# Self attention's output projections of seven token blocks: four products of four 128 by 128 by 512 matmuls, or seven half-size products combined in place

## The chip, the cores and the metric

The kernel runs on one core of one Trainium2 chip. The metric is the device time of one execution in microseconds (us); lower is better. All arithmetic is float32.

## The reference, cut to what matters

The program is an encoder over a short context (77 tokens), then a decoder layer over x of shape (2, 2048, 512) with 16 heads of 32. The step that changes is the output projection of the decoder's causal self attention, with its residual:

```
yn = _ln(y, dec_n1_s, dec_n1_b)
y = y + _mha(yn, yn, dec_sa_in_w, dec_sa_in_b, dec_sa_out_w, dec_sa_out_b, sb)
...
out = jnp.einsum('bhqk,bhkd->bhqd', attn, v)
out = out.transpose(0, 2, 1, 3).reshape(Bq, Tq, D)
return out @ w_out.T + b_out
```

So 2 x 2048 rows of attention output, 512 wide, are multiplied by a 512 by 512 weight; a bias row and the residual y are added. After it come cross attention and a feed-forward layer.

## The kernel before, in words

**Blocks and units.** The 4096 tokens are eight blocks of 512, written (b, m): batch b in 0..1 and m in 0..3; here they are also called block 0 to 7. A block's self attention is 16 units: four groups g of four heads, and in each group four tiles t of 128 query tokens. A unit of block m has 4m+t+1 key tiles. It is worked through by `scores` (L374 matmuls into PSUM banks; VectorE copies the scores out with a running maximum, L383, and adds the bias near the diagonal, L390; L399 makes the negated maximum), `exps` (ScalarE, L404), `turn` (TensorE transposes, L424, copied out by ScalarE, L430, or VectorE, L428) and `values` (L452). Scores of a unit are computed up to two units ahead.

**Order.** Nothing is scheduled by a tool: each engine runs its instructions in the order of the program text. At the start of unit n the function `slot(n)` emits, in this order, the closures in `light[n]`, the jobs in `jobs[n]`, then those in `late[n]`. Jobs are TensorE products: q (`q_job`, L215), k and v of each block, and the output projection. Light and late work is normalisation, loads and GpSimd sums. Every load and store is issued by SyncE's queue (SP), in program order; a load that waits for its buffer holds up all later ones. `load_next` fetches a job's weights ahead, at most three in the ring `wqk` of three 256 KB buffers.

**Half-size products, already there.** For blocks with m > 0, k and v are made not by four full products but by seven products of half-size factors (`part_job`, L1024 to L1063): one 256 by 256 quarter of the weight, or a sum of quarters made once (`wc_sums`, `wc_store`, kept in DRAM as `sa_k`, `sa_v`), times one quarter of the block's 512 by 512 input or a sum of quarters (T1 to T4, made by GpSimd in `token_sums`, L956). Each product is four matmuls of 256 columns (L1038) into one bank, and its result is copied or added into one or two quarters of the output.

**The output projection.** `out_job(b, m, t)` (L246 to L257) takes the weight held in the 1 MB tile `wbt` and the block's four oT tiles (one per group; 512 features by 512 tokens altogether; GpSimd has divided them by the softmax sums at L489). It makes one tile of 128 tokens: four matmuls of 512 columns (L251), one VectorE add of the residual tile (L254), one store (L255). The residual tile was loaded (L262) and had the bias row `bo` added by GpSimd (L266) a unit before. Block x's four out jobs stand in units 6, 7, 8, 9 of the next block (7 to 10 where the next block starts a batch); those of the last block come after the units. `wbt` holds v's full weight for the first block of each batch and the output weight otherwise. `fold_job` (L1065) folds v's bias through the output weight into `bo`, once, in block 1.

**Neighbours in the same units.** Units 5 to 8 load the normalisation input of the block after next (`norm_load`, tag xt, two buffers, L275); unit by unit GpSimd scales it (`norm_center`, L286, L293) and TensorE transposes it (`norm_turn`, L305). In block 2 GpSimd also makes sums of feed-forward weights (`w2_sums`, L956 on `pp`), in block 6 of others; in blocks 4 and 5 the first block's cross attention is woven in (`first_cross`).

Of the kernel before, what the change touches and what calls it, by code (L numbers as in the profile page):

```python
# [10 lines left out]
F32 = mybir.dt.float32  # L11
AF = mybir.ActivationFunctionType
ALU = mybir.AluOpType
# [4 lines left out]
P = 128  # L18
# [36 lines left out]
def tile_encoder_decoder(ctx: ExitStack, tc: tile.TileContext, ins, out):  # L55
# [103 lines left out]
    with (  # L159
# [34 lines left out]
        nTs, qTs, ots, sums_of = {}, {}, {}, {}  # L194
        wbig, xs, xr = {}, {}, {}

# [38 lines left out]
        def v_job(b, m, t):  # L235
            def run(w):
                mm = bank()
                for c in range(NC):
                    nc.tensor.matmul(
                        mm, nTs[b, m][:, c, ts(t, P)], w[:, c, :], start=(c == 0), stop=(c == NC - 1)  # L240
                    )
                nc.vector.tensor_copy(vv[:, m * TB + t, :], mm)

            return lambda: big_w("v"), run, False

        def out_job(b, m, t):  # L246
# [9 lines left out]

            return lambda: big_w("o"), run, False  # L257

# [178 lines left out]
        def values(pair):  # L437
# [18 lines left out]
            if keep:  # L456
                return
            if (b, m, g) not in ots:
                ots[b, m, g] = in_turn("oT", oT_all)
            o = ots[b, m, g]  # L460
# [529 lines left out]

        sa_d = {k: dram.tile([4, P, D], F32, name=f"sa_{k}", tag=f"sa_{k}") for k in "kv"}
        sa_from = {"k": D, "v": 2 * D}
        kstep = sm.tile([P, 2], F32, name="kstep", tag="kstep", bufs=1)
# [13 lines left out]
        def token_sums(b, m):  # L1007
# [3 lines left out]
            for name in ("T1", "T2", "T3", "T4"):  # L1011
                sum_n(name, lambda n: of_nT(b, m, n))

        def part_job(kind, b, m, i):
            name, by = PARTS[i]

            def load():
                w = sb.tile([P, NC, P], F32, name="wqk", tag="wqk", bufs=3).rearrange("p c o -> p (c o)")
                w = w.rearrange("p (c o) -> p c o", c=2)
                if name[0] == "S":  # L1020
                    src = sa_d[kind][int(name[1]) - 1].rearrange("p (c o) -> p c o", c=2)
                else:
                    src = quarter("dec_sa_in_wT", int(name[1]) - 1, int(name[0]) - 1, sa_from[kind])
                nc.sync.dma_start(w, src)  # L1024
# [61 lines left out]
        for x, (b, m) in enumerate(blocks):  # L1086
# [28 lines left out]
            for t in range(TB):  # L1115
                end = x == len(blocks) - 1
                out_at = u + NU + (2 if end else 7 if m == NMB - 1 else 6) + t
                jobs[out_at].append(out_job(b, m, t))
                if not end:
                    (light if x else late)[out_at - 1].append(lambda b=b, m=m, t=t: residual(b, m, t))  # L1120
                elif t < 2:
                    light[u + NU - 1].append(lambda b=b, m=m, t=t: residual(b, m, t))
                if x:
                    held = x == 1 and t >= 2
# [141 lines left out]
        light[len(units) - 5].append(early_loads)  # L1266
        light[len(units) - 1].append(last_loads)


# [576 lines left out]
```

## Time and profile before

| what | value |
|---|---|
| three runs, us | 2768.12, 2771.48, 2767.57; median 2768.12 |
| profiled execution, us | 2771.65 |
| its span, first to last instruction, us | 2769.9 |
| granted TensorE clock, mean | 0.995 |
| TensorE busy / VectorE / ScalarE / GpSimd, us | 2724.6 / 1807.0 / 1538.8 / 915.6 |
| SP's dynamic DMA queue | 358.18 MB, 41.4% of 16 engines' span |

How to read it: PE is TensorE's matmuls, PEld its weight loads, DVE VectorE, ACT ScalarE, POOL GpSimd, SPq the DMA queue of SyncE. A float32 matmul shows as two records. A group line gives source line, engine, operation, output<-input, shapes, the number of records, busy us, mean ns of one, and the idle time before them with what ended it. A timeline line gives start in us, length in us, engine, line, operation and count; idle time and its releaser stand in brackets. Records of matmuls overlap: the length of one is not the time for which it holds the engine; that is read from start to start.

### The profile page before, as it was taken

The page shows a single profiled execution, that of the slowest core. Times are in us where ns is not written, and L with a number is a line of the kernel's source. Part 1 is how long each engine was busy: PE and PEld are TensorE (multiplying, and loading weights), DVE is VectorE, ACT ScalarE, POOL GpSimd, SP SyncE. Part 2 cuts the span into 40 slices and gives each one's busy share as a digit, 9 for nine tenths or more (in the row PEclk, how much of TensorE's full clock was granted, in tenths as well). Part 3 has the DMA queues.
Part 4 walks back from the last instruction along what each step waited for, and adds up shares of the span by engine and source line. Part 5 has one row for each costly group of instructions (what it writes and reads, how often), then busy time and mean ns, then how long its engine had stood idle before and what let it go on. Part 6 is the DMA issues. An engine that isn't in the chain of part 4 may idle for free.

```text
span 2769.9 us, 67113 instructions
## 1 busy us (share of the span) xinstructions
PE 2724.6 (98%) x26294; PEld 2154.4 (78%) x26294; DVE 1807.0 (65%) x5312; ACT 1538.8 (56%) x2993; POOL 915.6 (33%) x777
## 2 busy tenths in 40 slices
PE   9999999999999999999999999999999999999998
PEld 5577776677776567676677777898989898989898
DVE  5775587787776587677687783556464646464645
ACT  3444567667777557677667786444444444444431
POOL 1501135300100413213200003364646464646456
PEclk9999999999999999999999999999999999999999
DMA  8433345311112422233211004565657564656465
GB/s 225 141 97 113 106 124 178 118 55 48 47 40 70 130 78 68 72 100 115 95 50 35 29 29 158 184 227 160 225 160 239 170 223 162 222 162 222 148 225 183
DMA packets 282254, 362.47 MB, mean 131 GB/s; under 512 B 39072, under 2 KB 156624, under 8 KB 281810
## 3 DMA queue, kind: packets, MB, share of 16 engines
q1 hardware_dynamic: 281938, 358.18, 41.4%
q8 instruction: 208, 3.41, 0.5%
q14 instruction: 108, 0.88, 0.1%
HBM read 314.49 MB, written 43.59 MB: 129 GB/s over the span
## 4 chain that ended last, share of the span: by engine, by line
PE 89%; DVE 4%; ACT 3%; issue 1%; POOL 1%; DMA 1%; SPq 0%; POOLq 0%; DVEq 0%; ACTq 0%
PE psum L424 17%; PE psum L1516 14%; PE psum L1545 12%; PE psum L374 9%; PE psum L452 8%; PE psum L1038 4%; PE psum L251 4%; PE psum L215 4%; PE psum L1676 3%; PE psum L1633 3%; ACT pp L404 3%; DVE pp L383 2%; PE psum L860 2%; PE psum L830 1%; PE psum L868 1%
## 5 line engine op out<-in xcount | busy, mean ns | idle before, releaser
L404 ACT ACTIVATE pp<-pp,nm 128x128 f32<-128x128 f32 (+15 forms) x512 | 611.8, 1201 | 34.5 <-DVE nm L399 34.0
L383 DVE TENSOR_SCALAR_CACHE_REDUCE pp<-psum 128x512 f32<-128x512 f32 (+3 forms) x1024 | 555.5, 591 | 75.0 <-PE psum L374 73.4
L424 PE MATMUL psum<-ident,pp 128*128 128x128 f32 x4352 | 536.4, 278 | 20.2 <-ACT pp L404 13.5
L430 ACT COPY pts<-psum 128x512 f32<-128x512 f32 (+2 forms) x736 | 386.5, 580 | 298.9 <-PE psum L424 258.0
L424 PEld LDWEIGHTS psum<-ident,pp 128*128 128x128 f32 x4352 | 478.5, 142 | 79.4 <-issue 24.9
L374 PE MATMUL psum<-kT,q 32*128 32x512 f32 (+3 forms) x2560 | 321.6, 559 | 4.6 <-ACT nT L310 2.6
L452 PEld LDWEIGHTS psum<-pts,vv 128*32 128x32 f32 x8704 | 226.7, 110 | 122.5 <-DVE pp L383 67.5
L428 DVE COPY pts<-psum 128x512 f32<-128x512 f32 (+3 forms) x400 | 249.5, 654 | 106.6 <-PE psum L424 104.4
L1545 PE MATMUL psum<-pp 128*128 128x128 f32 x2560 | 304.5, 276 | 1.9 <-POOL pp L956 1.6
L1545 PEld LDWEIGHTS psum<-pp 128*128 128x128 f32 x2560 | 296.3, 192 | 8.6 <-issue 2.8
L452 PE MATMUL psum<-pts,vv 128*32 128x128 f32 x8704 | 279.5, 276 | 6.7 <-DVE pp L383 4.2
L956 POOL TENSOR_TENSOR pp<-pp 128x512 f32<-128x512 f32 x159 | 212.6, 1354 | 126.5 <-DMA pp<-in_dec_ff_wT_dram 66.5
L1516 PE MATMUL psum<-vv,pp 128*128 128x256 f32 x1024 | 236.2, 381 | 0.0
L374 PEld LDWEIGHTS psum<-kT,q 32*128 32x128 f32 x2560 | 138.4, 183 | 125.6 <-issue 53.6
L1516 PEld LDWEIGHTS psum<-vv,pp 128*128 128x128 f32 x1024 | 190.3, 190 | 25.8 <-issue 0.5
L390 DVE CUSTOM_DVE_ANT_0 pp<-psum,bias 128x256 f32<-128x256 f32 (+1 forms) x512 | 196.2, 411 | 13.8 <-PE psum L374 13.6
L1529 DVE TENSOR_TENSOR kT<-kT,psum 128x512 f32<-128x512 f32 x96 | 65.8, 686 | 191.1 <-PE psum L1516 190.9
L1516 PE MATMUL psum<-nT,pp 128*128 128x256 f32 x768 | 174.1, 380 | 0.0
L1532 ACT ACTIVATE kT<-kT,vecs 128x256 f32<-128x256 f32 x192 | 87.0, 501 | 156.6 <-DVE kT L1529 155.9
L489 POOL TENSOR_TENSOR oT<-rirows,oT 128x512 f32<-128x512 f32 x30 | 38.4, 1280 | 377.9 <-DMA rirows<-rec 269.8
L1516 PEld LDWEIGHTS psum<-nT,pp 128*128 128x128 f32 x768 | 144.2, 190 | 20.3 <-issue 1.6
L266 POOL TENSOR_TENSOR xr<-xr,row_dec_sa_out_b 128x512 f32<-128x512 f32 x30 | 38.2, 1274 | 352.9 <-DMA xr<-in_x_dram 304.9
(243 smaller groups left out, 3907.5 us busy)
## 6 DMA issues: line engine op xcount, KB each, us to landing
pp<-w_d SPq DMA_DIRECT2D x520, 256.0 KB
pp<-in_dec_ff_wT_dram SPq DMA_DIRECT2D x112, 256.0 KB
wqk<-in_dec_sa_in_wT_dram SPq DMA_DIRECT2D x76, 256.0 KB
bias<-tzg SPq DMA_DIRECT2D x128, 128.0 KB
pp<-wo_d SPq DMA_DIRECT2D x56, 256.0 KB
vv<-in_enc_ff_wT_dram SPq DMA_DIRECT2D x8, 1024.0 KB
xr<-in_x_dram SPq DMA_DIRECT2D x32, 256.0 KB
vv<-y SPq DMA_DIRECT2D x32, 256.0 KB
```

The source lines that it names most:

```text
L215: nc.tensor.matmul(mm, w[:, c, :], nTs[b, m][:, c, :], start=(c == 0), stop=(c == NC - 1))
L374: nc.tensor.matmul(banks[r][:, : kn * P], q[rows4(r), ts(t, P)], kT[rows4(r), g, k0 * P : (k0 + kn) * P], start=True, stop=True,)
L383: nc.vector.tensor_scalar(p[:, k0 : k0 + far], s[:, :far], 1.0, None, ALU.mult, ALU.max, accum_out=st["mx"][:, r, c : c + 1],)
L390: nc.vector.tensor_tensor_reduce(p[:, k0 + far : i + 1], s[:, far:kn], near[:, 2 - (kn - far) :], 1.0, LOWEST, ALU.add, ALU.max, accum_out ...
L404: nc.scalar.activation(p, p, AF.Exp, bias=nm, accum_out=to)
L424: nc.tensor.transpose(pt[:, ts(x, P)], state[n]["p"][r][:, k], ident)
L428: nc.vector.tensor_copy(pts[:, : len(load), :], pt[:, :w])
L430: nc.scalar.copy(pts[:, : len(load), :], pt[:, :w])
L452: nc.tensor.matmul(ot[rows4(r)], vv[:, k, ts(g * HC + r, HD)], got.pop((n, k, r)), start=k == k0 and (whole or not begun), stop=k == k1 - ...
L956: engine.tensor_tensor(out, a, b, ALU.subtract)
L1516: nc.tensor.matmul(mm[:, ts(f, TOK)], a[:, c, ts(f, P)], b[:, c, :], start=fresh and f == 0 and c == 0, stop=c == 1, skip_group_check=True,)
L1545: nc.tensor.matmul(psum[:, bank_i, ts(col, P)], lhs[:, c, :], w[:, c, :], start=fresh and k in (0, 3) and c == 0, stop=c == 3, skip_group_ ...
```

## The change

For the seven blocks that are not the last, the four out jobs are replaced by seven `part_job`s of a new kind "o", in units 6, 6, 7, 7, 8, 8, 8 of the next block (7 to 9 for block 3). Their results go into quarters of `wbt`, which is now the accumulator; the output weight is loaded in quarters through the `wqk` ring, its sums from a new DRAM tile `sa_o` (made once, unit 12). GpSimd makes T1 and T2 of oT in two xr tiles, T3 and T4 over quarters of oT itself, and at the end adds `bo` and the `wbt` tile to each residual tile (`out_done`), which is then stored. The last block keeps `out_job`; its weight is loaded into `wbt` in the last unit.

```
def of_o(b, m, name):
    if name in ("T1", "T2"):
        return o_tiles[b, m][int(name[1]) - 1].rearrange("p (c o) -> p c o", c=2)
    name = {"T3": "12", "T4": "11"}.get(name, name)
    r, c = int(name[0]) - 1, int(name[1]) - 1
    i = ots_at[b, m, 2 * r]
    return oT_all[:, i : i + 2, ts(c, TOK)]

def out_sums(b, m):
    o_tiles[b, m] = [sb.tile([P, D], F32, name="xr", tag="xr", bufs=2) for _ in range(2)]
    for name in ("T1", "T2", "T3"):
        sum_n(name, lambda n: of_o(b, m, n))

def out_done(b, m, t):
    x1 = xr.pop((b, m, t))
    nc.gpsimd.tensor_tensor(x1, x1, bo, ALU.add)
    nc.gpsimd.tensor_tensor(x1, x1, wbt[:, t, :], ALU.add)
    nc.sync.dma_start(y1[b][m][:, t, :], x1)
```

```
 in part_job:
+                if kind == "o":
+                    return wbt[:, 2 * c : 2 * c + 2, ts(r, TOK)]
...
-                n, mm = of_nT(b, m, by), bank()
+                n, mm = of_o(b, m, by) if kind == "o" else of_nT(b, m, by), bank()
...
 in the loop over blocks:
                 out_at = u + NU + (2 if end else 7 if m == NMB - 1 else 6) + t
+                if not end:
+                    if t:
+                        continue
+                    for k, part in ((0, 1), (0, 6), (1, 7), (1, 4), (2, 2), (2, 5), (2, 3)):
+                        jobs[out_at + k].append(part_job("o", b, m, part))
+                    late[out_at - 2].append(lambda b=b, m=m: out_sums(b, m))
+                    late[out_at].append(lambda b=b, m=m: sum_n("T4", lambda n: of_o(b, m, n)))
+                    for k in range(TB):
+                        late[out_at + 2 + k // 2].append(lambda b=b, m=m, k=k: residual_load(b, m, k))
+                        light[out_at + 3 + k // 2].append(lambda b=b, m=m, k=k: out_done(b, m, k))
+                    continue
                 jobs[out_at].append(out_job(b, m, t))
-                if not end:
-                    (light if x else late)[out_at - 1].append(lambda b=b, m=m, t=t: residual(b, m, t))
...
-        for n, kind in ((2, "k"), (5, "v")):
-            light[n].append(lambda kind=kind: wc_sums("dec_sa_in_wT", True, spare, sa_from[kind]))
+        for n, kind in ((2, "k"), (5, "v"), (12, "o")):
+            light[n].append(lambda kind=kind: wc_sums(sa_name[kind], True, spare, sa_from[kind]))
             late[n + 1].append(lambda kind=kind: wc_store(sa_d[kind], spare))
...
+        light[len(units) - 1].append(lambda: big_w("o"))
+        light[NMB * NU - 2].append(lambda: big_w("v"))
```

Order of the seven products (part number: weight factor, input factor, where the result goes): 1: 11, 11, copied to quarter 11 by ScalarE; 6: S2, T2, with 11 to 12; 7: S3, T3, with 12 to 22; 4: 22, T4, with 22 to 21; 2: 12, 21, added to 11; 5: S1, T1, added to 22 and 12; 3: S4, 22, added to 12. All but the first are VectorE adds.

More of the change, by code (lines that the diff above doesn't have):

```diff
@@ L194, in tile_encoder_decoder @@
         nTs, qTs, ots, sums_of = {}, {}, {}, {}
-        wbig, xs, xr = {}, {}, {}
+        wbig, xs, xr, ots_at = {}, {}, {}, {}
         def small_w(c0, name="dec_sa_in_wT"):
@@ L458, in values @@
             if (b, m, g) not in ots:
+                ots_at[b, m, g] = count["oT"] % oT_all.shape[1]
                 ots[b, m, g] = in_turn("oT", oT_all)
@@ L988, in wc_store @@
                 nc.sync.dma_start(dst[i], z[4 + i])
-        sa_d = {k: dram.tile([4, P, D], F32, name=f"sa_{k}", tag=f"sa_{k}") for k in "kv"}
-        sa_from = {"k": D, "v": 2 * D}
+        sa_d = {k: dram.tile([4, P, D], F32, name=f"sa_{k}", tag=f"sa_{k}") for k in "kvo"}
+        sa_from = {"k": D, "v": 2 * D, "o": 0}
+        sa_name = {"k": "dec_sa_in_wT", "v": "dec_sa_in_wT", "o": "dec_sa_out_wT"}
         kstep = sm.tile([P, 2], F32, name="kstep", tag="kstep", bufs=1)
@@ L1022, in load @@
                 else:
-                    src = quarter("dec_sa_in_wT", int(name[1]) - 1, int(name[0]) - 1, sa_from[kind])
+                    src = quarter(sa_name[kind], int(name[1]) - 1, int(name[0]) - 1, sa_from[kind])
                 nc.sync.dma_start(w, src)
@@ L1117, in tile_encoder_decoder @@
                 out_at = u + NU + (2 if end else 7 if m == NMB - 1 else 6) + t
+                if not end:
[9 more added lines that the diff above has]
+                    continue
                 jobs[out_at].append(out_job(b, m, t))
[L1119 to L1121 removed]
+                if t < 2:
                     light[u + NU - 1].append(lambda b=b, m=m, t=t: residual(b, m, t))
+            for t in range(TB):
                 if x:
```

10 lines of the change are left out of this document (8 added, 2 removed).

## The prediction

> **What bounds the kernel now.** I read the page first, then busy time by stretches, the waits of TensorE, groups by form, and the timeline around the out jobs.
>
> ```profile
> PE 89%; DVE 4%; ACT 3%; issue 1%; POOL 1%; DMA 1%; SPq 0%; POOLq 0%; DVEq 0%; ACTq 0%
> ```
> ```profile
> core 0: us, PE busy (x) PEld busy (x) DVE busy (x) ACT busy (x) POOL busy (x), PEclk, DMA share, GB/s
> 402.00:600.00 198.00, 192.46 (x2206) 138.58 (x2208) 148.98 (x504) 141.55 (x243) 72.39 (x60) 0.99 0.42 128
> 600.00:860.00 260.00, 257.79 (x3269) 192.77 (x3258) 207.48 (x690) 202.11 (x308) 20.73 (x16) 1.00 0.13 40
> ```
> ```profile
> PE psum L424 <- ACT pp L404: 13.5, 14, 2.4
> PE psum L452 <- DVE pp L383: 4.2, 14, 0.3
> ```
>
> TensorE is 89% of the chain that ended last. The two stretches are blocks 2 and 3. In both TensorE is the fullest engine, but in block 3 VectorE has 80% and ScalarE 78%, so a unit with little TensorE work in it can turn to them. TensorE's largest wait is 13.5 us for the exponentials (L404), 14 times. So TensorE time taken out of a unit is gained where VectorE and ScalarE keep up, and turns into a wait where they don't.
>
> **The products.** Timeline of TensorE in block 2 (a 512-column out job), then a stretch of block 0 (256-column half-size products), then transposes of 128 columns:
>
> ```profile
> 458.38 3.60 PE L251 MATMUL psum<-wbig,oT 128*128 128x512 f32 x8
> 461.91 1.14 PE L374 MATMUL psum<-kT,q 32*128 32x512 f32 x8
> ```
> ```profile
> 158.69 1.89 PE L1038 MATMUL psum<-wqk,nT 128*128 128x256 f32 x8
> 160.42 1.89 PE L1038 MATMUL psum<-wqk,xt 128*128 128x256 f32 x8
> 162.24 1.14 PE L374 MATMUL psum<-kT,q 32*128 32x512 f32 x8
> ```
> ```profile
> 478.52 3.71 PE L424 MATMUL psum<-ident,pp 128*128 128x128 f32 x32
> 482.17 2.00 PE L374 MATMUL psum<-kT,q 32*128 32x512 f32 x16
> ```
>
> From start to start an out job holds TensorE for 461.91 - 458.38 = 3.53 us. A half-size product holds it for 160.42 - 158.69 = 1.73 us, and 1.82 us where scores follow, so the switch costs 0.09. A 128-column record takes 3.65 / 32 = 114 ns, a 256-column one 1.73 / 8 = 216 ns: the slope is 0.80 ns a column, the part that doesn't shrink with the width 13 ns at most.
>
> Per block: removed 4 x 3.53 = 14.12 us; added 7 x 1.73 plus three switches of 0.09 = 12.38 us. That is 1.74 us less, and over seven blocks **-12.2 us**, the term that carries the forecast. Bounds: with 13 ns for each of the 24 added records a block it could be 0.3 x 7 = 2 us less were those not already in the 1.73; I keep -12.2.
>
> **The other engines' share.**
>
> ```profile
> L254 DVE TENSOR_TENSOR xr<-psum,xr 128x512 f32<-128x512 f32 x30 | 20.8, 692 | 62.6 <-PE psum L251 59.0 <-issue 2.4 <-POOL xt L293 1.3
> L1063 DVE TENSOR_TENSOR vv<-psum,vv 128x512 f32<-128x512 f32 x24 | 16.0, 689 | 13.9 <-PE psum L1038 13.9
> L266 POOL TENSOR_TENSOR xr<-xr,row_dec_sa_out_b 128x512 f32<-128x512 f32 x30 | 38.2, 1274 | 352.9 <-DMA xr<-in_x_dram 304.9 <-DVE mx L390 36.9 <-DVE pts L428 10.4
> ```
> ```profile
> L430 ACT COPY pts<-psum 128x512 f32<-128x512 f32 (+2 forms) x736 | 386.5, 580 | 298.9 <-PE psum L424 258.0
> ```
>
> VectorE: seven adds of 0.69 us (part 5 has two, part 1 none) for four: +2.1 us a block. They come while TensorE works on products: the last three parts ask 4 x 0.69 = 2.8 us of VectorE in 5.2 us of TensorE. Hidden; uncovered it would be 2.1 x 7 = 14 us. GpSimd: four sums and four more adds of 1.27 us, +10.2 us a block; it was busy 72.4 of 198 us in block 2, the fullest. What TensorE needs of it are T2 and T4. The tightest place for T2 is block 2, behind the feed-forward sums:
>
> ```profile
> 447.77 2.08 POOL L956 TENSOR_TENSOR kT<-pp,kT 128x384 f32<-128x384 f32 x2
> ```
>
> They end at 449.8, three sums at 453.6, and the first product starts at 458.38: hidden, with 5 us to spare. T4 has a whole unit. `out_done` waits for a load and stands ahead of `norm_center` of the fourth tile in GpSimd's queue, and its stores hold up SP (scale rows, bias, next loads). I count 4.2 us from the start of the third pair of units to the residual loads, 3.0 for landing (below) and four adds: 12.3 us, and 15 with `norm_center`. The turn that needs it comes two units later, 24 us or more, by the first and the last of block 0's out jobs, three units and 41 us apart:
>
> ```profile
> 241.91 3.70 PE L251 MATMUL psum<-wbig,oT 128*128 128x512 f32 x8
> ...
> 282.90 3.60 PE L251 MATMUL psum<-wbig,oT 128*128 128x512 f32 x8
> ```
>
> So that is hidden too. The one-time sums for `sa_o` (5.1 us of GpSimd, 2 MB) lie in unit 12, where nothing waits for GpSimd: nothing.
>
> [...]
>
> **Weights that now come late.** Seven quarter loads a block join SP's queue. SP and GpSimd in block 1, SP and TensorE in block 2:
>
> ```profile
> 258.60 0.38 SPq L262 DMA_DIRECT2D xr<-in_x_dram  x1
> ```
> ```profile
> 261.58 1.27 POOL L266 TENSOR_TENSOR xr<-xr,row_dec_sa_out_b 128x512 f32<-128x512 f32 x1 [2.99 <-DMA xr<-in_x_dram]
> ```
> ```profile
> 487.78 0.60 PE L305 MATMUL psum<-ident,xt 128*128 128x128 f32 x4
> 488.22 3.60 PE L251 MATMUL psum<-wbig,oT 128*128 128x512 f32 x8
> ```
> ```profile
> 488.45 0.33 SPq L275 DMA_DIRECT2D xt<-in_x_dram  x1
> 488.83 0.43 SPq L1024 DMA_DIRECT2D wqk<-in_dec_sa_in_wT_dram  x1
> ```
>
> A 256 KB load lands 3.0 us after its issue starts. Six parts are fetched a unit or more ahead. The seventh (part 3) is issued only in its own unit, behind a `norm_load` that waits for a transpose in that unit: as here at 488.83, 0.6 us into the product time. It lands at 491.8; two products end at 488.22 + 3.46 = 491.7. So 0.1 to 0.5 us of wait; I take 0.3 in six blocks, **+1.8 us**. For block 3's outputs there is a second place:
>
> ```profile
> 920.14 0.86 SPq L920 DMA_DIRECT2D vv<-in_dec_ca_out_wT_dram  x1
> 921.05 0.83 SPq L262 DMA_DIRECT2D xr<-in_x_dram  x1
> ```
> ```profile
> 925.10 3.70 PE L251 MATMUL psum<-wbig,oT 128*128 128x512 f32 x8
> 933.98 0.66 PE L305 MATMUL psum<-ident,xt 128*128 128x128 f32 x4 [1.42 <-POOL xt L293]
> ```
> ```profile
> 928.71 1.29 POOL L266 TENSOR_TENSOR xr<-xr,row_dec_sa_out_b 128x512 f32<-128x512 f32 x1 [4.62 <-DMA xr<-in_x_dram]
> ```
>
> Behind a 1 MB load the 256 KB took 7.6 us. Part 6's weight takes that place: it lands near 928.6 and is wanted at 925.10 + 1.73 = 926.8, +1.8 us. The same late residual made GpSimd and then TensorE wait 1.42 us; that residual is now loaded later, so this wait goes. **+0.4 us** together.
>
> **Where the gain isn't collected.** Blocks 2 and 6 have units of 9 to 12 key tiles, in which the exponentials are just in time. Block 2's unit 10 has no job at all, before and after:
>
> ```profile
> 464.64 3.39 PE L424 MATMUL psum<-ident,pp 128*128 128x128 f32 x29 [0.54 <-ACT pp L404]
> ```
> ```profile
> 521.83 0.33 PE L424 MATMUL psum<-ident,pp 128*128 128x128 f32 x1 [2.45 <-ACT pp L404]
> 523.28 4.73 PE L424 MATMUL psum<-ident,pp 128*128 128x128 f32 x29 [1.12 <-ACT pp L404]
> ```
> ```profile
> 520.00:530.00 10.00, 6.93 (x53) 5.68 (x57) 3.88 (x15) 8.12 (x12) 9.77 (x10) 0.83 1.02 286
> ```
>
> With a job, unit 6 waits 0.54 us (464.64). Without one, unit 10 waits 3.57 us, and the granted clock falls to 0.83 in the ten us around, in which the same 29 records take 4.73 us, not 3.39. The change puts the products in units 6, 7 and 8, so unit 9 loses its job. Its VectorE work is then what limits it and unit 10: in 402 to 600 VectorE has 149 of 198 us, more in these units. I take half of the 1.74 lost, and 0.6 for part 1's ScalarE copy (L430's mean is 580 ns) ahead of unit 6's exponentials: 1.5 us in each of two blocks, near the row with a job since unit 9 is smaller than unit 10. **+3.0 us.** Bounds: nothing (the wait is absorbed), to 3.57 + 1.34 a block as in unit 10, 9.8 us.
>
> **Sum.** -12.2 + 1.8 + 0.4 + 3.0 = **-7.0 us**. The profiled execution took 2771.65 us, so 2764.6 for it; it lay 3.5 us above the median 2768.12, and the median of the changed kernel is put at 2761 us, 0.26% less. A measurement of this kernel can tell about 0.2%, 5.5 us, from no change.
>
> **Rivals.**
> 1. *Units without a job eat the gain.* Unit 9 of blocks 2 and 6 behaves as unit 10 (9.8 us instead of 3.0), perhaps a little in blocks 3 and 7 too. Then -0.2 us: 2768, between 2763 and 2772. For it: VectorE and ScalarE at 80% in block 3. Against: unit 9 has 10 key tiles, unit 10 has 11, and block 3's unit 10, without a job, waits little:
>
> ```profile
> 783.24 1.12 PE L374 MATMUL psum<-kT,q 32*128 32x512 f32 x2 [0.34 <-ACT nT L310]
> ```
>
> 2. *Late weights: slower.* Part 3's load in six blocks and others land as the load at 921.05, 7.6 us and not 3.0: 4.6 us more, each time on TensorE's path. 6 x 4.6 = 28 us: 2789. The gain is gone when the wait reaches 7 / 6 = 1.2 us more than counted, that is when landing takes 4.2 us. For it: SP is one queue, and blocks 1, 2 and 6 carry 1 MB loads. Against: at 258.60 and 488.83 those had landed; from 4.2 us on, only a 1 MB load just ahead does it.
> 3. *Narrow products don't scale.* If a record's own length counted, not start to start:
>
> ```profile
> L251 PE MATMUL psum<-wbig,oT 128*128 128x512 f32 x256 | 115.5, 594 | 0.0
> L1038 PE MATMUL psum<-wqk,nT 128*128 128x256 f32 x144 | 34.0, 379 | 0.0
> ```
>
> 56 records of 379 ns are 21.2 us against 32 of 594 ns, 19.0: +2.2 a block, +15 us, 2783. [...] The starts above (1.73 against 3.53 us) speak against it here.
> 4. *More than forecast.* Unit 10's wait shrinks, the clock isn't lost (1.34 us twice), part 3 is in time: -12 to -16 us, 2754.
>
> **How the numbers follow.** Forecast, 2756 to 2762.6: 0.52. Rival 4, below 2756: 0.08. Rival 1, and the forecast's upper edge, 2762.6 to 2773.6: 0.24. Rival 2: 0.14, half of it below 2780. Rival 3: 0.02. So faster by over 0.2%: 0.60; within 0.2%: 0.24; slower: 0.16. Range 2754 to 2776: some 0.04 is left out below, 0.12 above.
>
> **What would show it.** In the changed profile the new L1064 products (from `wqk`, `oT` and `xr`) should start 1.73 us apart; if 2 us or more, rival 3. Waits of TensorE's L1064 for the weight loads should total 4 us or less; 10 or more is rival 2. In blocks 2 and 6 TensorE's waits for L404 in units 9 and 10 should grow by 1 to 2 us a block; 5 or more is rival 1. GpSimd should be busy some 75 us more, with no wait of TensorE for L957. The forecast is wrong if VectorE's adds delay the scores (waits for L383 well over 4.2 us), or if SP, held up by `out_done`'s stores, delivers the bias late.

## The result, and the profile after

The changed kernel takes 2760.06 us in the median of six runs (2757.42 to 2761.86), the kernel before 2768.01 in six (2767.57 to 2771.48). That is 8.0 us less; 7.0 less was forecast, to 2761. The ratio on record is 0.9965, with a 95% interval from 0.9955 to 0.9975: 6.9 to 12.5 us less. The profiled execution of after took 2760.2 us, its span 2758.4, 11.5 less than the span before.

The page of after, busy time (us, share of the span, instructions) and the head of the chain:

```profile
PE 2712.3 (98%) x26462; PEld 2185.1 (79%) x26462; DVE 1821.2 (66%) x5333; ACT 1541.2 (56%) x3000; POOL 992.2 (36%) x837
...
PE 90%; DVE 4%; ACT 3%; issue 1%; DMA 1%; POOL 1%; SPq 0%; POOLq 0%; DVEq 0%; ACTq 0%
```

TensorE is busy 12.3 us less than before (2724.6), VectorE 14.2 more and GpSimd 76.6 more: the forecast's 12.2, 2.1 x 7 and "some 75". TensorE is still nine tenths of the chain. VectorE and GpSimd, which got more work, keep their shares of it, 4% and 1%.

TensorE's waits of after (waiting line and what ended it: us in total, times, longest), in the order of the view:

```profile
PE psum L424 <- ACT pp L404: 14.2, 14, 2.5
PE psum L452 <- DVE pp L383: 4.5, 15, 0.3
PE psum L374 <- ACT nT L310: 3.8, 4, 2.1
...
PE psum L1064 <- DMA wqk<-sa_o: 0.3, 2, 0.2
```

Against before: 13.5 has become 14.2, 4.2 has become 4.5, and the third line was 2.6 in 3 times. The weight loads show 0.3 us in two waits. No line names GpSimd's sums over `oT` or its residual adds (L1034, L1035). The one line on L957 with GpSimd is 1.6 us for the sums of feed-forward weights, as before (then L956).

The products on TensorE's timeline of after, in blocks 1, 2 and 4 (start, length):

```profile
267.33 1.89 PE L1064 MATMUL psum<-wqk,oT 128*128 128x256 f32 x8
269.06 1.89 PE L1064 MATMUL psum<-wqk,xr 128*128 128x256 f32 x8
271.11 1.97 PE L1064 MATMUL psum<-wqk,oT 128*128 128x256 f32 x8 [0.15 <-DMA wqk<-sa_o]
...
487.81 1.89 PE L1064 MATMUL psum<-wqk,xr 128*128 128x256 f32 x8
489.74 1.97 PE L1064 MATMUL psum<-wqk,oT 128*128 128x256 f32 x8
...
947.13 1.89 PE L1064 MATMUL psum<-wqk,oT 128*128 128x256 f32 x8
948.95 0.93 PE L374 MATMUL psum<-kT,q 32*128 32x384 f32 x8
```

From start to start a product takes 1.73 us. The third of unit 8, whose weight is asked for last, starts 2.05 us after the second in block 1 and 1.93 in block 2. So it was late by 0.3 and 0.2 us, though the bracket shows 0.15 and nothing: a stall of less than a row's own overlap is read from starts, not from brackets. Over the seven blocks these delays come to 1.0 us (0.32, 0.20, 0.33, 0, 0, 0.17, 0). The load behind the one in block 2, on SP's queue of after:

```profile
486.31 0.34 SPq L275 DMA_DIRECT2D xt<-in_x_dram  x1
486.70 0.42 SPq L1048 DMA_DIRECT2D wqk<-sa_o  x1
```

It stands behind a `norm_load` that waited for a transpose, as forecast, and so starts 0.6 us after the unit's first product (486.08). The third product starts 3.0 us later. In blocks 1, 3 and 6 it is the same, 3.0 to 3.1 us; in blocks 4 and 5 the load starts 2.5 us or more ahead of the unit's first product.

**Where the time came from, by blocks.** The same instruction in both profiled executions, at a place behind each block's seven products (starts in us; products of q, L215, and for blocks 5 and 7 the groups of L424 and L452 that wait 0.54 and 0.34 us in both):

| mark behind the products in | before | after | after less before | since the last mark |
|---|---|---|---|---|
| (ahead of those in block 1) | 228.21 | 226.83 | -1.38 | -1.38 |
| block 1 | 308.44 | 305.80 | -2.64 | -1.26 |
| block 2 | 638.55 | 636.15 | -2.40 | +0.24 |
| block 3 | 796.31 | 793.31 | -3.00 | -0.60 |
| block 4 | 1032.46 | 1027.61 | -4.85 | -1.85 |
| block 5 | 1236.15 | 1229.04 | -7.11 | -2.26 |
| block 6 | 1361.53 | 1353.49 | -8.04 | -0.93 |
| block 7 | 1638.43 | 1628.74 | -9.69 | -1.65 |

The seven blocks gain 8.3 us. Three of them fall well short of the 1.74 of the forecast, 2, 3 and 6, and block 5 shows more than it. The first line and the 1.8 us after the last one are no part of the change, as will be seen. In blocks 2 and 3 the rows are these (TensorE of after):

```profile
462.48 3.38 PE L424 MATMUL psum<-ident,pp 128*128 128x128 f32 x29 [1.00 <-ACT pp L404]
...
518.42 0.47 PE L424 MATMUL psum<-ident,pp 128*128 128x128 f32 x1 [2.45 <-ACT pp L404]
519.87 5.73 PE L424 MATMUL psum<-ident,pp 128*128 128x128 f32 x29 [0.97 <-ACT pp L404]
...
765.08 0.91 PE L374 MATMUL psum<-kT,q 32*128 32x384 f32 x4 [0.98 <-ACT nT L310]
```

Unit 6 (462.48) waits 1.00 us where it waited 0.54. Unit 10 waits as before, but the 29 transposes behind the wait now take 5.73 us, not 4.73: a loss of 1.0 that sits in no instruction of the change. And in block 3 scores in unit 9, which lost its job, wait 0.98 us that were not there. By the starts the 16 records of these scores take 3.60 us (762.32 to 765.92), where they took 2.76 before (766.16 to 768.92): 0.84 us more.

Why unit 6 waits longer, on ScalarE's timeline of after:

```profile
457.49 1.46 ACT L404 ACTIVATE pp<-pp,nm 128x1408 f32<-128x1408 f32 x1
...
458.94 0.57 ACT L1075 COPY wbig<-psum 128x512 f32<-128x512 f32 x1
459.41 1.47 ACT L404 ACTIVATE pp<-pp,nm 128x1408 f32<-128x1408 f32 x1
```

The first part's copy into `wbt` (L1075) stands between the second and the third exponential. The same picture in unit 10, 57 us later, where a part that the change doesn't touch, the copies of the normalised tile (L310), stands at that place:

```profile
515.43 1.49 ACT L310 ACTIVATE nT<-psum,vecs 128x128 f32<-128x128 f32 x4
516.80 1.48 ACT L404 ACTIVATE pp<-pp,nm 128x1408 f32<-128x1408 f32 x1
518.16 0.21 ACT L404 ACTIVATION_READ_ACCUMULATOR pp<-pp,nm 128x1 f32 x1
```

The third exponential ends at 518.37, and the transpose that waited 2.45 us starts at 518.42.

Block 4, on SP's queue and then on TensorE of after:

```profile
914.75 0.84 SPq L921 DMA_DIRECT2D vv<-in_dec_ca_out_wT_dram  x1
915.69 0.99 SPq L1048 DMA_DIRECT2D wqk<-sa_o  x1
```
```profile
922.12 1.99 PE L1064 MATMUL psum<-wqk,oT 128*128 128x256 f32 x8
923.95 1.89 PE L1064 MATMUL psum<-wqk,xr 128*128 128x256 f32 x8
...
926.66 0.48 PE L374 MATMUL psum<-kT,q 32*128 32x128 f32 x2 [0.39 <-ACT nT L310]
...
930.24 0.60 PE L305 MATMUL psum<-ident,xt 128*128 128x128 f32 x4
```

Part 6's weight does stand behind the 1 MB load, as the forecast had it, but it is issued 6.4 us ahead of the first product, and the second product starts 1.83 us after the first, without a bracket. Why SP is earlier shows in its waits of before:

```profile
SPq L205 <- PE psum L239: 6.6, 1, 6.6
```

L205 is the load of the output weight into `wbt`, which waited 6.6 us until v's products (L239) were done with that tile. The changed kernel has no such load there, and its 1 MB load starts 7.4 us ahead of the first product, not 5.0. (This is read from the traces; no run tests it.)

The 1.42 us wait of L305 for GpSimd is gone (930.24); with a smaller wait just ahead of it, TensorE gets 1.7 us there by the starts. Two stalls took its place: the scores in the rows above take 1.30 us from start to start, not 0.43 (the bracket shows 0.39 of the 0.87), and a group of scores at 973 us takes 0.62 more.

Block 5, TensorE of before, then of after:

```profile
1124.50 1.82 PE L374 MATMUL psum<-kT,q 32*128 32x512 f32 x16
...
1136.54 2.35 PE L452 MATMUL psum<-pts,vv 128*32 128x128 f32 x48
1138.82 4.06 PE L424 MATMUL psum<-ident,pp 128*128 128x128 f32 x28
```
```profile
1117.99 3.83 PE L374 MATMUL psum<-kT,q 32*128 32x512 f32 x16
...
1130.97 1.52 PE L452 MATMUL psum<-pts,vv 128*32 128x128 f32 x48
1132.42 3.28 PE L424 MATMUL psum<-ident,pp 128*128 128x128 f32 x28
```

Two things meet here. The scores at 1117.99 stand where the fourth out job stood just ahead of them, in unit 9. They hold TensorE for 3.77 us from start to start, not 1.92; of these 1.85 us, 0.9 come back within the next 10 us, so about 1.0 is lost. Then, in before, the granted clock fell (0.51 from 1137 to 1139, 0.82 from 1139 to 1143; 1.00 in after), and the last two rows took 1.6 us longer. That second part is no gain of the change.

The change's adds on GpSimd and VectorE of after, grouped by form (records, then busy us and mean ns of one, then idle time before them and its ends):

```profile
L1034 POOL TENSOR_TENSOR xr<-xr,row_dec_sa_out_b 128x512 f32<-128x512 f32 x28 | 35.8, 1279 | 79.8 <-DMA xr<-in_x_dram 63.5 <-DVE pp L383 16.3
L1035 POOL TENSOR_TENSOR xr<-xr,wbig 128x512 f32<-128x512 f32 x28 | 35.7, 1276 | 14.3 <-DVE wbig L1089 12.1
L1089 DVE TENSOR_TENSOR wbig<-psum,wbig 128x512 f32<-128x512 f32 x28 | 18.7, 688 | 14.9 <-PE psum L1064 14.3 <-ACT pp L404 0.6
```

Both of GpSimd's adds cost 1.28 us, VectorE's accumulations 0.69, as forecast from the rows of before.

**The clock.** The granted clock is not the same from one execution to the next at the same place. Ten us from 110 on, in before, in after and in the experiment with spare transposes of below (start and end; busy us of PE, PEld, DVE, ACT, POOL; clock; DMA share; GB/s):

```profile
110.00:120.00 10.00, 7.89 (x67) 6.73 (x66) 5.00 (x19) 5.50 (x18) 5.00 (x4) 0.66 0.01 2
```
```profile
110.00:120.00 10.00, 7.89 (x68) 6.25 (x67) 5.74 (x21) 6.26 (x21) 6.92 (x6) 0.83 0.01 2
```
```profile
110.00:120.00 10.00, 7.90 (x69) 5.37 (x68) 5.51 (x22) 5.92 (x20) 7.26 (x6) 1.00 0.00 2
```

TensorE is busy for the same time in all three, but the clock is 0.66, 0.83 and 1.00, right behind a TensorE wait of 2.1 us (the longest of the L310 waits above, at 113), and at the table's first mark they stand in that order: 228.21, 226.83 and 224.81. From the scores that end that wait (113.79, 113.59 and 113.25) to the mark it is 114.4, 113.2 and 111.6 us. So 1.2 of the 1.38 us of the first line go with the clock, at a place that the change doesn't reach; the other 0.2 are there by 11 us. The same happens in unit 10 of blocks 2 and 6, and in the last unit of block 7, where the 29 transposes took 5.05 us before and 3.38 after. Of the 11.5 us between the two spans, 1.4 and 1.7 are such luck, and 8.3 are the blocks'. Within these 8.3 the clock took 1.0 us in block 2 and gave 1.6 in block 5 and 0.1 in block 6, so the change itself is worth about 7.6 us in these two executions.

### The profile page after: what moved, and what is told of

It is laid out like the page before. It is cut to its first block, busy times and chain, and to the rows that moved or that the text cites. A ratio compares the mean times of both kernels' runs of the same rounds, so it can differ in the third digit from the quotient of the medians.

```text
span 2758.4 us, 67720 instructions
## 1 busy us (share of the span) xinstructions
PE 2712.3 (98%) x26462; PEld 2185.1 (79%) x26462; DVE 1821.2 (66%) x5333; ACT 1541.2 (56%) x3000; POOL 992.2 (36%) x837
## 4 chain that ended last, share of the span: by engine, by line
PE 90%; DVE 4%; ACT 3%; issue 1%; DMA 1%; POOL 1%; SPq 0%; POOLq 0%; DVEq 0%; ACTq 0%
PE psum L424 18%; PE psum L1554 14%; PE psum L1583 12%; PE psum L374 9%; PE psum L452 9%; PE psum L1064 7%; PE psum L215 4%; PE psum L1714 3%; PE psum L1671 3%; ACT pp L404 3%; PE psum L861 2%; DVE pp L383 2%; PE psum L831 1%; PE psum L869 1%; PE psum L586 1%; PE psum L806 1%
## 5 line engine op out<-in xcount | busy, mean ns | idle before, releaser
L424 PE MATMUL psum<-ident,pp 128*128 128x128 f32 x4352 | 534.7, 278 | 20.8 <-ACT pp L404 14.2
L424 PEld LDWEIGHTS psum<-ident,pp 128*128 128x128 f32 x4352 | 476.7, 141 | 79.8 <-DVE pp L383 24.0
L452 PEld LDWEIGHTS psum<-pts,vv 128*32 128x32 f32 x8704 | 225.7, 110 | 122.6 <-DVE pp L383 68.5
L452 PE MATMUL psum<-pts,vv 128*32 128x128 f32 x8704 | 278.0, 275 | 7.0 <-DVE pp L383 4.5
L957 POOL TENSOR_TENSOR pp<-pp 128x512 f32<-128x512 f32 x159 | 212.8, 1355 | 126.0 <-DMA pp<-in_dec_ff_wT_dram 66.0
L1591 ACT COPY oT<-psum 128x128 f32<-128x128 f32 x56 | 15.0, 268 | 238.8 <-PE psum L1583 238.8
```

The costliest lines, as they stand in the source:

```text
L424: nc.tensor.transpose(pt[:, ts(x, P)], state[n]["p"][r][:, k], ident)
L452: nc.tensor.matmul(ot[rows4(r)], vv[:, k, ts(g * HC + r, HD)], got.pop((n, k, r)), start=k == k0 and (whole or not begun), stop=k == k1 - ...
L957: engine.tensor_tensor(out, a, b, ALU.subtract)
```

## The experiments

Theory A, stated after the result: the gain is TensorE time, and the part of the 12.2 us that is missing was lost in units where ScalarE's queue is the last to be ready (unit 6 of blocks 2 and 6, unit 10) or where the job went away (unit 9). Its rivals: VectorE's scores set the pace, so that such waits only move (B); the gain comes from the residuals being handled elsewhere, and TensorE time is not the term (C); the difference is luck of the clock. Experiments 1 to 4 ran together, 5 to 8 together, 9 to 11 together, and 12 alone, each group with its own runs of the kernel before, to which the ratios refer; kernels of different groups are compared by these ratios. Each kernel ran 5 to 11 times.

### 1. The third part's product in unit 9

```
-  for k, part in ((0, 1), (0, 6), (1, 7), (1, 4), (2, 2), (2, 5), (2, 3)):
+  wide = x != 3
+  for k, part in ((0, 1), (0, 6), (1, 7), (1, 4), (2, 2), (2, 5), (2 + wide, 3)):
...
-      late[out_at + 2 + k // 2].append(...)
-      light[out_at + 3 + k // 2].append(...)
+      late[out_at + 2 + wide + k // 2].append(...)
+      light[out_at + 3 + wide + k // 2].append(...)
```

> The changed kernel with product 3 moved from unit 8 to unit 9 (all blocks but block 3's outputs), the residual loads and final adds one unit later. Theory A (the gain is TensorE time, and it is lost where a unit loses its job: ScalarE's exponentials in blocks 2 and 6, ScalarE's normalisation copies in block 3): the 0.98 us wait in block 3's unit 9 goes, and each of blocks 2, 3 and 6 gives 0.5 to 1.5 us back: 2757 to 2759 us against 2760.1. Rival B (where the products stand doesn't matter, the missing gain went to late weights or VectorE): 2760 us within 0.5, and the waits stay.

Measured: 2760.89 us, ratio 0.9965 (0.9952 to 0.9979): the same as the changed kernel. The wait of 0.98 us in block 3 is gone, but its trace has new ones (TensorE):

```profile
550.42 3.13 PE L424 MATMUL psum<-ident,pp 128*128 128x128 f32 x24 [0.78 <-ACT kT L1071]
```

A miss for A by the time. By the marks, giving unit 9 a job back wins 1.0 us in block 3 and, without the clock, 1.0 in block 5 (the scores there take 2.05 us again, not 3.77) and next to nothing in blocks 2 and 6. New stalls take it: 1.3 us around the row above and 0.6 in block 4, for a load; and the clock in block 5 fell as in before, 1.6 us.

### 2. Before, with unit 9 emptied

The kernel before, its fourth out job moved from unit 9 to unit 8, its residual loaded two units ahead:

```
-  jobs[out_at].append(out_job(b, m, t))
+  packed = t == TB - 1 and not end
+  jobs[out_at - packed].append(out_job(b, m, t))
+  if packed:
+      late[out_at - 2].append(lambda b=b, m=m, t=t: residual(b, m, t))
...
```

> The kernel before, with its fourth out job moved from unit 9 to unit 8 (its residual loaded after unit 7's job); nothing else. It takes the cover from unit 9 without any of the new products. Theory A: slower than before by 1 to 4 us, 2769 to 2772, with the same 0.98 us wait in block 3's unit 9 as in the changed kernel and more lost in blocks 2 and 6. Rival B: 2768 us within 0.5.

Measured: 2770.72 us against 2769.78, ratio 1.0004 (0.9995 to 1.0013), about 1 us. The empty unit 9 makes the same wait in block 3 without any half-size product (TensorE):

```profile
768.95 0.91 PE L374 MATMUL psum<-kT,q 32*128 32x384 f32 x4 [0.98 <-ACT nT L310]
```

In block 5 it makes the same two groups of scores of 3.83 us each as after (1125.09 and 1134.30). So both losses belong to where the jobs stand, not to what they are. By the starts in after the empty unit 9 costs 0.8 us in block 3 and 1.0 in block 5; the medians of these two experiments, which can't tell 2 us, put it between nothing and about 1 us.

### 3. An eighth product of the same size

The changed kernel with one more product of four 256-column matmuls in each of the seven blocks; its result is not read.

```
+  jobs[out_at + 3].append((lambda: None, lambda w: spare_product(), False))
```

> The changed kernel with one more product of four matmuls of 256 columns, on other data and not used, in unit 9 of each of the seven blocks (unit 10 for block 3's outputs). It costs TensorE 1.73 us a block and nothing else. If TensorE's time is what ends everywhere: +12.1 us, 2772. Theory A: it is free or nearly so in blocks 2, 3 and 6, whose unit 9 waits anyway, and costs 1.73 in the other four: +7 to +9 us, 2767 to 2769. Rival C (the gain of the change isn't TensorE time but came from the residual handling): 2760 to 2762.

Measured: 2772.49 us, ratio 1.0007 (0.9998 to 1.0015), where the changed kernel has 0.9965: 11.6 us more by the ratios, the full TensorE time of seven products being 12.1. Its profiled execution, the shortest of its eleven at 2768.6, shows 8.0 us more by the blocks' marks, 9.0 without the clock of unit 10: 1.5 to 1.7 in each of blocks 1, 2, 6 and 7, 0.7 to 1.0 in blocks 3, 4 and 5. So the time is nearer the full price, and the trace has A's total, but not its places: unit 9 of blocks 2 and 6 is not free, that of block 5 is in part. C has little room: 12 us of TensorE time put back, with everything else in its new place, undo the gain. No run handles the residuals in the new way with the old products; in block 4, where the trace shows what that brought (1.7 us), two stalls took most of it.

### 4. Twice the change's work on GpSimd

`out_done` adds the bias row three times, not once (the output is another one: the row comes in three times). That is 8 more adds of 1.28 us a block, 10.2 us, as much as the change itself added.

```
-  nc.gpsimd.tensor_tensor(x1, x1, bo, ALU.add)
+  for _ in range(3):
+      nc.gpsimd.tensor_tensor(x1, x1, bo, ALU.add)
```

> The changed kernel with the bias row added three times instead of once to each residual tile (the output changes by two bias rows in these blocks): eight more GpSimd adds of 1.27 us a block, 10.2 us, as much again as the change added. The prediction's step (GpSimd is hidden): 2760 us within 1. Rival D (GpSimd's queue, with SP's stores behind it, is on the path): each block later by some of the 10.2 us, 2765 us or more, with waits of TensorE for L293 or for the bias.

Measured: 2778.46 us, ratio 1.0031 (1.0020 to 1.0043), by the ratios 18 us over the changed kernel. TensorE's waits have a new first line, and the longest of the three is in block 4 (waits, then timeline; L1065 here is L1064 of after):

```profile
PE psum L1065 <- POOL xt L957: 15.6, 3, 10.3
```
```profile
987.49 3.78 PE L1065 MATMUL psum<-xt,wqk 128*128 128x256 f32 x8 [10.30 <-POOL xt L957]
```

The sums of the next block's input (L957) queue on GpSimd behind `out_done`, and that block's k and v products wait for them. The forecast costed GpSimd's added 10.2 us a block at nothing, and the changed kernel has no such wait. But the cover is less than as much again: in block 4 of after these sums end at 973.05 and the first of the products starts at 977.60, 4.5 us later.

### 5. The first part's copy on VectorE

```
+  elif i == 1 and kind == "o":
+      ve.tensor_copy(d["11"], got)
```

> The changed kernel, but the first product's copy into its quarter is made by VectorE and not by ScalarE. Theory A (part of the gain is lost to ScalarE, where the copy of 0.57 us stands ahead of the third of four exponentials in unit 6 of blocks 2 and 6): TensorE's wait there falls from 1.00 to about 0.54 us, 0.9 us for the kernel: 2759, ratio to before 0.9962. Theory B (VectorE's scores, L383, set the pace of these blocks): the copy moves 0.69 us onto VectorE in seven units, and the time is the same or up to 2 us longer, 2760 to 2762. Both are within what five rounds can tell; the trace's wait in unit 6 is what tells them apart.

Measured: 2756.85 us (2756.67 to 2757.86), ratio 0.9952 (0.9939 to 0.9964); the changed kernel beside it (experiment 8) 2761.91, 0.9968 (0.9956 to 0.9981). Unit 6 of block 2 on TensorE:

```profile
460.92 3.39 PE L424 MATMUL psum<-ident,pp 128*128 128x128 f32 x29 [0.52 <-ACT pp L404]
```

The wait is 0.52 us again, in block 6 too: 0.96 us that A claimed, and no wait took its place. The medians differ by 5, and the two profiled executions by 2.45 us (2757.00 and 2759.45). Of these, 1.0 is the copy, 0.9 was lost to the clock ahead of the table's first mark in experiment 8 and not here, and 0.55 in unit 10 of block 2 likewise. The rest of the medians' difference is not explained, and the two intervals overlap.

### 6. Spare transposes in the waits of unit 10

The changed kernel with 18 and 8 transposes whose result is not read, between the second and third and the third and fourth transposes that wait in unit 10 of blocks 2 and 6 (units 42 and 106). They shift later lines by two.

```
+  if (k, n) in ((0, 42), (0, 106)) and r > 1:
+      warm((18, 8)[r - 2])
   nc.tensor.transpose(pt[:, ts(x, P)], state[n]["p"][r][:, k], ident)
```

> The changed kernel, plus 18 and 8 transposes whose result nobody reads, put where TensorE waits 2.45 and 0.97 us for the exponentials in unit 10 of blocks 2 and 6; at 114 ns each they need 2.05 and 0.91 us, so they fit in the waits. Theory A, clock part (the granted clock falls because TensorE idles there): the 29 transposes behind the waits take 3.4 us and not 4.7 to 6.1, so 1.3 to 2.7 us are won twice: -2.6 to -5 us, 2755 to 2758, ratio 0.995 to 0.996. Rival (the clock falls for another cause, or the wait only moves): the 29 transposes still take over 4.5 us, and the time is that of the changed kernel, 2760, or up to 1 us more.

Measured: 2756.45 us (2753.36 to 2756.66), ratio 0.9950 (0.9936 to 0.9964). TensorE in unit 10, then the stretch around it:

```profile
516.35 0.33 PE L426 MATMUL psum<-ident,pp 128*128 128x128 f32 x1 [0.48 <-ACT pp L404]
517.80 3.38 PE L426 MATMUL psum<-ident,pp 128*128 128x128 f32 x29 [0.25 <-ACT pp L404]
```
```profile
515.50:525.50 10.00, 9.15 (x127) 7.42 (x126) 5.23 (x17) 9.17 (x15) 7.00 (x6) 1.00 0.48 154
```

The waiting transposes still start when their exponentials are done, since idle time was filled and none was added; the 29 behind them take 3.38 us in block 2 and 3.39 in block 6, against 5.46 and 5.45 in the changed kernel beside it. 4.1 us come from doing useless work, within the 2.6 to 5 that A expected; the medians differ by 5.5. The granted clock in that stretch is 1.00, where after has 0.66 in the same ten us. The clock theory holds, its rival falls.

### 7. The normalised tile's copies on VectorE

```
-  on = nc.vector if x == 1 and t % 2 else nc.scalar
+  on = nc.vector if x == 1 and t % 2 or m == 3 and t == 3 else nc.scalar
```

> The changed kernel, but the four copies of the normalised input's last tile (L310, 1.49 us on ScalarE between the second and the third exponential of unit 10, blocks 2 and 6) are made by VectorE. Theory A (ScalarE's queue sets unit 10): the third and fourth exponentials come 1.4 us earlier, the wait of 2.45 us falls to about 1.0, and with the clock kept the gain is 1.4 to 4 us twice: 2752 to 2757, ratio 0.994 to 0.996. Theory B (VectorE's scores set the pace): VectorE takes these copies in the midst of the next unit's scores, the wait moves to there, and the time stays at 2759 to 2762.

Measured: 2756.71 us (2756.15 to 2760.52), ratio 0.9953 (0.9941 to 0.9966). TensorE in unit 10 of block 2:

```profile
516.86 0.48 PE L424 MATMUL psum<-ident,pp 128*128 128x128 f32 x1 [1.06 <-ACT pp L404]
518.31 5.95 PE L424 MATMUL psum<-ident,pp 128*128 128x128 f32 x29 [0.98 <-ACT pp L404]
```

2.45 us became 1.06, and 1.07 in block 6: 2.8 us won, with no new wait in these blocks. The clock was still lost in this execution (5.95 us, and 4.95 in block 6). So ScalarE's order sets unit 10, not VectorE's scores: B falls for this unit.

### 8. The changed kernel again

> The changed kernel itself once more, as the base of the three kernels beside it on the same chip: 2760 us, ratio 0.9965, within 0.001 of it.

Measured: 2761.91 us (2759.45 to 2764.07), ratio 0.9968 (0.9956 to 0.9981).

### 9. Three edits together

The edits of experiments 5 and 7, and those of experiment 6 with fewer transposes:

```
+  if (k, n) in ((0, 42), (0, 106)) and r > 1:
+      warm((8, 8)[r - 2])
```

> The changed kernel with the first product's copy on VectorE, the copies of the normalised input's last tile in blocks 3 and 7 on VectorE, and 8 and 8 unused transposes (not 18 and 8, since the longer wait is now 1.06 us) in the two waits of unit 10 of blocks 2 and 6. Theory A (ScalarE's queue in units 6 and 10, and the clock lost after the idle time): the gains add where they are different places: 0.9 us for the copy, 2.8 us for the earlier exponentials, 2.6 to 4 us for the clock, so 6 to 8 us under the changed kernel: 2752 to 2755, ratio to before 0.9935 to 0.995. Theory B (the waits only move): no better than the best of the three alone, 2756.

Measured: 2752.77 us (2752.66 to 2753.25), ratio 0.9934 (0.9921 to 0.9948). TensorE in unit 10 of block 2:

```profile
516.24 0.33 PE L426 MATMUL psum<-ident,pp 128*128 128x128 f32 x1 [0.19 <-ACT pp L404]
517.69 3.39 PE L426 MATMUL psum<-ident,pp 128*128 128x128 f32 x29 [0.25 <-ACT pp L404]
```

By the ratios this is 9.4 us under experiment 8 and 8.6 under the first measurement of after. By the blocks' marks it is 8.2 us under experiment 8, and the traces of the three edits alone account for 1.0, 2.8 and 4.1, 7.9 in all: where a trace shows them, the gains add. The medians of the three alone (5.1, 5.2 and 5.5 us) come to twice that, and do not.

### 10. A fourth edit, in block 3

As 9, with experiment 1's edit for block 2's outputs alone, so that the third part's product stands in unit 9 of block 3:

```
-  wide = x != 3
+  wide = x == 2
```

> As the kernel with the three edits, and the third part's product of block 2's outputs goes from unit 8 to unit 9 of block 3, with its residual adds a unit later. Theory A (a unit that lost its job waits; in block 3 the wait of 0.98 us for the copies out of the bank that the scores want): this wait goes, 0.6 to 1 us less than with the three edits. Rival (the wait moves to another place): the same time. Too little to be told by the medians; the trace tells it.

Measured: 2751.38 us (2750.71 to 2752.25), ratio 0.9929 (0.9917 to 0.9942). The wait of 0.98 us is gone from the trace and none replaces it there. By the marks block 3 is 0.8 us shorter than in experiment 9. It is the fastest kernel of the study, 19 us under the kernel before; the step from 9 to 10 alone, 1.4 us, is within what the ratios leave open.

### 11. Before, with the spare transposes

The edit of experiment 6 in the kernel before:

```
+  if (k, n) in ((0, 42), (0, 106)) and r > 1:
+      warm((18, 8)[r - 2])
```

> The kernel before, with the same 18 and 8 unused transposes in the waits of unit 10 of blocks 2 and 6. Theory (the clock falls after the idle time in either kernel, and by chance more or less): the 29 transposes take 3.4 us here too, not 4.7 and 5.7, so 2766 to 2767, ratio 0.9985 to 0.999. Against the changed kernel with the same transposes (2756.5) this leaves the change itself without the clock: theory A expects 8 to 10 us (the sum of the blocks' gains), the forecast's sum 7.

Measured: 2764.54 us (2762.57 to 2769.69), ratio 0.9980 (0.9971 to 0.9989). TensorE, block 2:

```profile
521.97 3.39 PE L426 MATMUL psum<-ident,pp 128*128 128x128 f32 x29 [0.25 <-ACT pp L404]
```

The kernel before wins from this as well, and more than expected: 5.9 us by the medians, of which the trace has 3.6 in unit 10 of blocks 2 and 6. Between experiments 11 and 6, with the clock held in unit 10 of both, the change is worth 0.9980 - 0.9950 of 2770, 8.3 us: its gain is not luck of the clock in unit 10.

### 12. Spare transposes in the last unit too

As 10, with 4 and 14 more in unit 127, the last of block 7:

```
-  if (k, n) in ((0, 42), (0, 106)) and r > 1:
-      warm((8, 8)[r - 2])
+  if (k, n) in ((0, 42), (0, 106), (0, 127)) and r > 1:
+      warm(((8, 8) if n < 127 else (4, 14))[r - 2])
```

> The kernel with the four edits, plus 4 and 14 unused transposes (0.46 and 1.60 us) in the waits of 0.54 and 1.65 us of the last unit of the last block, behind which the same kind of 29 transposes took 3.4 us in some profiles and 5.1 in others. Clock theory: they take 3.4 us in the profile, the median falls by 0 to 1.7 us against the four edits (2751.4, ratio 0.9929), and the times of single executions lie within 2 us of each other. Rival (the last unit's clock has another cause): the 29 transposes take 5 us in the profile again, or the time is longer.

Measured: 2752.44 us (2751.45 to 2753.95), ratio 0.9936 (0.9922 to 0.9949). TensorE in the last unit, and what follows 8 us later:

```profile
1664.67 3.38 PE L426 MATMUL psum<-ident,pp 128*128 128x128 f32 x29
...
1675.95 7.17 PE L1559 MATMUL psum<-nT,pp 128*128 128x256 f32 x32 [0.48 <-DVE oT L469]
```

The transposes take 3.38 us (5.05 in the profile of experiment 10), and the wait of 1.65 us ahead of them is filled; yet the median is no better, and the runs spread over 2.5 us, more than the 2 expected. In the two profiled executions the trace shows why. This one was 1.6 us behind experiment 10 at the table's first mark already (228.09 and 226.50), since the clock in the ten us from 110 on was 0.66 and not 0.83. It keeps that distance to the last unit, wins the 1.67 us there, and gives 0.56 back, most of it in the new wait of 0.48 us. So the edit works where it stands; whether the median gains by it is open.

## Why the prediction was right, point by point

**The products: -12.2 us.** Right: TensorE is busy 12.3 us less, products start 1.73 us apart, and experiment 3 pays nearly the full price by the medians (three quarters of it in its trace) when it adds the same amount. By the starts it is a little less: in block 7, where nothing waits, the gain is 1.65 us and not 1.74, 11.6 in seven blocks, since taking the fourth job out of unit 9 frees 3.43 us and not 3.53. Rival 3, that narrow products don't scale, is out: start to start (1.73 us), not the records' lengths (1.89), is what a product costs here.

**VectorE and GpSimd: nothing.** Right in size and in being hidden. For GpSimd the forecast's reason was too easy: it looked at T2, T4 and `norm_center`, while what is waited for first when GpSimd gets later is the next block's token sums (10.3 us in experiment 4). Nor did the added GpSimd time make VectorE's adds longer, as far as a mean can show it: the new adds of L1089 take 688 ns with GpSimd 76.6 us busier, where L254's took 692 and L1063's 689 before.

**Late weights: +1.8 us.** The mechanism was right (part 3, asked for in its own unit behind `norm_load`, landing 3.0 us after its issue), the size 1.0 us by the starts: four blocks and not six. Rival 2 priced the same wait at 28 us; it is out.

**Block 3's outputs: +0.4 us.** The step "part 6's load takes that place and is wanted 1.8 us too early" failed. The load was counted from where the residual's load stood before, and the forecast didn't see that SP stood still for 6.6 us there, at a load into `wbt` that the change takes away; part 6's weight was issued 6.4 us ahead of the first product. The other half was right: the 1.42 us wait for GpSimd went. But two stalls came (0.87 and 0.62 us by the starts), so block 4 kept 1.85 us where 1.74 and 1.7 were on offer.

**Gain not collected, blocks 2 and 6: +3.0 us.** Half right. The 0.6 us for part 1's copy ahead of the exponentials measured 0.46 in each block, and experiment 5 takes exactly that away. The other half, "unit 9 loses its job, VectorE limits it, half of 1.74 is lost", failed: units 9 and 10 of these blocks wait as before (2.45 and 0.97 against 2.45 and 1.12), and experiments 1 and 2 find no price there. The loss of an empty unit 9 came in blocks 3 and 5 instead, 0.8 and 1.0 us. For block 3 the forecast had called on the small wait of 0.34 at 783.24 as a sign of room; block 5 it didn't look at. That these 1.8 us equal the 1.74 that it took off for blocks 2 and 6 is luck.

**The sum.** The forecast had 12.2 - 1.8 - 0.4 - 3.0 = 7.0. The runs show 11.6 less 1.0 (part 3), 0.9 (part 1's copy twice) and 1.8 (unit 9 of blocks 3 and 5), and 0.2 more from block 4: 8.1. The clock adds 0.7 in the profiled pair (1.6 and 0.1 less 1.0): 8.8, where the table has 8.3. The 0.5 between lie in steps of 0.1 us that were not followed. The median moved by 8.0. So the mechanism that carries the forecast is right, and that the total came within 1 us is partly luck: the late weights (by 0.8), block 3's outputs (0.6) and the copy (0.3) cost less than forecast, the products gained 0.6 less, and the loss of unit 9 was right in size but in the wrong blocks.

Rival 1 (the empty units eat the gain) was the right worry at a fifth of its price and in other blocks. Rival 4 expected more because unit 10's wait might shrink; it didn't, since ScalarE's L310 copies stand in it, which the forecast had not read: it took VectorE's load as the limit there, and experiments 7 and 9 show ScalarE's order.

## What to carry to other kernels

Price a matmul from start to start, and take the whole difference in TensorE time as the first guess where TensorE is nine tenths of the chain; then look in the queue of each other engine for what a new instruction stands ahead of, since here a copy of 0.57 us ahead of an exponential cost 0.96 us in two blocks together (experiment 5), and 76.6 us of added work on GpSimd no new line with GpSimd in TensorE's waits. Before costing added work at nothing, find the next one in its queue and not only its own reader: doubling the work shows how thick the cover is (here a wait of 10.3 us came, experiment 4). And compare two profiles mark by mark, since their spans also differ by what the clock did at places that the change never touched (1.4 and 1.7 of 11.5 us here).

## What the hardware showed unexpectedly

Behind TensorE waits of 2.0 to 3.6 us in all, a group of 29 transposes took up to 2.7 us longer here (6.11 us in experiment 2 against 3.39). In unit 10 of blocks 2 and 6, after waits of 2.45 and 0.97 or 1.12 us with one transpose between, the same 29 transposes took from 4.71 to 6.11 us in every profile in which the waits were left as they were, never the 3.4 that they take elsewhere, and 5.95 and 4.95 after waits of 1.06 and about 1 us (experiment 7); after 0.54 and 1.65 us, in the last unit, they took 3.38 or 3.39 in some profiles and 4.84 to 5.05 in others; after 2.10 us at 113 the granted clock was between 0.66 and 1.00. In block 5, behind scores that took 4.41 us from start to start with a bracket of 0.2 alone, it fell in before (0.51 from 1137 to 1139) and in experiment 1, and not in experiments 3 and 11. With the waits filled they took 3.38 or 3.39 us each time, eleven times in five profiles.

So the length of the waits alone doesn't tell the loss: behind the same 0.54 and 1.65 us in the last unit the transposes took 5.05 us in experiments 9 and 10, and 3.38 in after and in experiment 6. What decides it, no run here shows.
